# A gate left in PSUM and bf16 parts read in place, in the edge messages of a graph network

## The chip, the core and the metric

The kernel runs on one core of a Trainium2 chip. The metric is the device time of one execution in microseconds (us). The core has five engines that run side by side, each in its own order: PE (TensorE, matrix products), DVE (VectorE), ACT (ScalarE), POOL (GpSimd) and SP (SyncE, which here only issues transfers). On-chip memory is SBUF (128 partitions) and PSUM[...].

## The reference

There are 6250 nodes with 64 features and 206250 edges, sorted by their target `dst`. Four layers follow one another, each on a normalised and rectified copy of the node features `x`, each added to `x`. The first, second and fourth are convolutions over the graph. The third is the one that the change touches; cut to its core, it computes

```
Vp = leaky_relu(leaky_relu(V) @ pAw + pAb) @ pBw + pBb      # nodes
x = relu(relu(E @ mlp_w1 + mlp_b1) @ mlp_w2 + mlp_b2)       # edges
scale = sigmoid(x @ Bw + Bb)
shift = x @ Cw + Cb
msg = scale * Vp[src] + shift
M = clip(msg, EPS, None) ** 2
mean = segment_sum(M, dst) / max(count, 1)
out = sqrt(mean)
```

So each edge fetches a row of `Vp` by its source node, multiplies it by a gate (the sigmoid), adds a shift, clips, squares, and is summed into its target node.

## The kernel before

The kernel first counts the edges between all pairs of nodes into a dense matrix `A` in fp8. The convolutions are then matrix products with `A`, in which the f32 node features are split into three bf16 parts. These stages lie before and after the one of interest and are not changed.

**The stage of the messages** goes over the edges in G = 202 groups. A group is 128 x 8 edges: 128 partitions, J = 8 edges in each, D = 64 features, so that a tile of a group is 128 x 512. The function `slot(i)` writes out one step of a software pipeline, in which different groups are at different steps: group i is fetched (`fetched`, L1351) and its edge features are turned (L1358), group i - 1 goes through the first edge layer, i - 2 through the second, i - 3 through `gates_and_shifts` (L1372), i - 4 (`M_AT`) becomes messages, i - 5 is summed (`summed`, L1404), and i - 6 is added to its nodes (`added_to_nodes`, L1413). The order on PE, ACT and DVE is just the order in which the code is written (`manual_schedule`); POOL and SP are ordered by the compiler's scheduler.

The steps of a group that matter here are these:

- `fetched` has POOL issue 8 indirect transfers (L1354), each of which fetches 128 rows of `Vp` by the edges' source indices, into the tile `v`, of which there are 4.
- `gates_and_shifts` has PE write `p_bc` in PSUM, the gate's and the shift's arguments beside one another for each edge, out of biases (L1376) and products (L1380). It takes two banks and there is one such tile, so PE can't begin the next group's before this one's is read.
- `gated` has ACT write the sigmoid of the gate's half into an SBUF tile `gate` (L1385).
- `clipped` has DVE multiply `gate` by `v` (L1389), add the shift out of `p_bc` (L1390), and take the maximum with EPS (L1391). L1390 is the last reader of `p_bc`.
- `squared` has ACT square the message twice: once rounded to bf16 into the first part of `m3` (L1396), once in f32 in place (L1397).
- In `slot`, DVE then compares the targets with the lanes of a window of nodes, which gives the 0/1 matrix `to` in bf16 (L1401), and subtracts the first part from the square (L1452); ACT rounds what is left to bf16, the second part (L1453); DVE subtracts that and writes the third part (L1464).
- `summed` has PE multiply `to` by the three parts, 8 products of 128 x 192 (L1408), which sum the messages of one target node.

Beside that, DVE and PE do other work in the same slots, handed out by `some_of`: the check that `A` is symmetric (`crossed`: PE turns pieces of `A`, L1260, and DVE compares them, L1266), and the next layer's first products (`partial`: PE at L748, DVE at L1285). SP loads for it `piece` (L1246) and `there` (L1253), and for the messages the edge features `e`, four slots ahead (L1348). Where a chunk of 7 blocks of nodes is complete, `finished` (L1320) takes roots and normalises it, six times within the stage and once at its end.

Of the kernel before, what the change touches and what calls it, by code (L numbers as in the profile page):

```python
# [8 lines left out]
F32 = mybir.dt.float32  # L9
BF16 = mybir.dt.bfloat16  # L10
FP16 = mybir.dt.float16
I32 = mybir.dt.int32
AF = mybir.ActivationFunctionType
# [3 lines left out]
P = 128  # L17
N = 6250
D = 64
# [6 lines left out]
J = 8  # L26
# [590 lines left out]
def fast(ctx, tc, bad, x, src, dst, edge_attr, W3, b3, W4, b4, w1, b1, w2, b2, Bw, Bb, Cw, Cb,  # L617
         pAw, pAb, pBw, pBb, out):

    nc = tc.nc  # L620
# [135 lines left out]
    with ExitStack() as ph:  # L756
# [73 lines left out]
        with ExitStack() as ps:  # L830
            psum = ps.enter_context(tc.tile_pool(name="ps0", bufs=1, space=PSUM, reuse_waits="tile"))
            p = psum.tile([P, SG, P], F32, name="p_a", bufs=2)
            nc.tensor.transpose(p[:D, 0, :], W3_sb, ident)
            nc.vector.tensor_copy(W3T, p[:D, 0, :])
            p = psum.tile([P, SG, P], F32, name="p_a", bufs=2)
# [43 lines left out]
            for c in range(GC):  # L879
# [8 lines left out]
                p = psum.tile([P, 1024], BF16, name="p_dig")  # L888
# [6 lines left out]
                if c % 9 == 8 or c == GC - 1:  # L895
                    c0 = c // 9 * 9
                    p = psum.tile([P, 512], F32, name="p_node")
# [19 lines left out]
            p = psum.tile([P, 512], F32, name="p_node")  # L917
# [7 lines left out]
            p = psum.tile([P, 512], F32, name="p_node")  # L925
# [288 lines left out]
    with ExitStack() as ph:  # L1214
        cpool, w1_d, w2_d, b1_c, b2_c, BC, BC_b, ones, src_g, lane, own, count = made.pop()
        mpool = ph.enter_context(tc.tile_pool(name="mpool", bufs=3, reuse_waits="tile"))
# [89 lines left out]
        def read_them():  # L1306
            while read:
                read.pop(0)()

        def some_of(n):  # L1310

            for _ in range(min(n, len(todo))):
                f, *args = todo.pop(0)
                if f is not here:
                    read_them()
                then = f(*args)
                if then:
                    read.append(then)
# [23 lines left out]
        BC_AT, M_AT, SUM_AT, ADD_AT = 3, 4, 5, 6  # L1342
        of = [{} for _ in range(G)]
        ends = [e + ADD_AT for e in ends]

        def loaded(g):
            of[g]["e"] = mpool.tile([P, J * D], F32, name="e", bufs=6)
            nc.sync.dma_start(of[g]["e"], edge_attr[g * P * J:(g + 1) * P * J, :].rearrange(  # L1348
                "(p j) f -> p (j f)", j=J))

        def fetched(g):  # L1351
            v = of[g]["v"] = mpool.tile([P, J, D], F32, name="v", bufs=4)
            for j in range(J):
                nc.gpsimd.indirect_dma_start(  # L1354
                    out=v[:, j, :], out_offset=None, in_=Vp_dram[:, :],
                    in_offset=bass.IndirectOffsetOnAxis(ap=src_g[:, g, j:j + 1], axis=0))

        def turned_edges(g):  # L1358
            p = of[g]["p_e"] = ps_a.tile([P, 512], F32, name="p_e")
            e = of[g].pop("e")  # L1360
            for k in range(J // 2):
                nc.tensor.transpose(p[:, k * P:(k + 1) * P], e[:, k * P:(k + 1) * P], ident)

        def layer(g, w, x, p):
            of[g][p] = ps_a.tile([P, 512], F32, name=p)
            nc.tensor.matmul(of[g][p], w, of[g].pop(x), start=True, stop=True)  # L1366

        def evicted(g, p, t, **how):
            of[g][t] = mpool.tile([P, 512], F32, name=t)
            nc.scalar.activation(of[g][t], of[g].pop(p), **how)  # L1370

        def gates_and_shifts(g):  # L1372
            p_bc = of[g]["p_bc"] = ps_a.tile([P, J, 2, D], F32, name="p_bc")
            h2 = of[g].pop("h2")
            for b in range(2):
                nc.tensor.matmul(p_bc[:, 4 * b:4 * b + 4].rearrange("p j o f -> p (j o f)"), ones,  # L1376
                                 BC_b, start=True, stop=False)
                for k in range(2):
                    q = 2 * b + k
                    nc.tensor.matmul(p_bc[:, 2 * q:2 * q + 2].rearrange("p j o f -> p (j o f)"),  # L1380
                                     h2[:, q * P:(q + 1) * P], BC, start=False, stop=(k == 1))

        def gated(g):
            gate = of[g]["gate"] = mpool.tile([P, J, D], F32, name="gate")
            nc.scalar.activation(gate, of[g]["p_bc"][:, :, 0, :], AF.Sigmoid)  # L1385

        def clipped(g):
            m = of[g]["m"] = mpool.tile([P, J, D], F32, name="m")
            nc.vector.tensor_mul(m, of[g].pop("gate"), of[g].pop("v"))  # L1389
            nc.vector.tensor_add(m, m, of[g].pop("p_bc")[:, :, 1, :])  # L1390
            nc.vector.tensor_scalar_max(m, m, EPS)  # L1391

        def squared(g):
            m = of[g]["m"]
            m3 = of[g]["m3"] = mpool.tile([P, J, 3, D], BF16, name="m3")
            nc.scalar.activation(m3[:, :, 0, :], m, AF.Square)  # L1396
            nc.scalar.activation(m, m, AF.Square)  # L1397

        def compared_nodes(g):
            to = of[g]["to"] = mpool.tile([P, P, J], BF16, name="to")  # L1400
            nc.vector.tensor_tensor(  # L1401
                to, count, lane[:, g, :].unsqueeze(1).to_broadcast([P, P, J]), op=OP.is_equal)

        def summed(g):  # L1404
            p = of[g]["p_s"] = ps_a.tile([P, 512], F32, name="p_s")[:, :3 * D]
            m3, to = of[g].pop("m3"), of[g].pop("to")
            for j in range(J):
                nc.tensor.matmul(p, to[:, :, j], m3[:, j].rearrange("p t f -> p (t f)"),  # L1408
                                 start=(j == 0), stop=(j == J - 1))

        begun = set()
# [1 line left out]
        def added_to_nodes(g):  # L1413

            r = mpool.tile([P, D], F32, name="r_s")
            nc.vector.tensor_reduce(r, of[g].pop("p_s").rearrange("p (t f) -> p f t", f=D),
                                    axis=AX.X, op=OP.add)
            for k, (b, q0, q1) in enumerate(halves(g)):
                part = own[:, q1 if k else q0, k:k + 1]
                if b in begun:  # L1420
                    nc.vector.scalar_tensor_tensor(H[:, b, :], r, part, H[:, b, :],
                                                   op0=OP.mult, op1=OP.add)
                else:
                    nc.vector.tensor_scalar(H[:, b, :], r, part, None, op0=OP.mult)
                    begun.add(b)
            return [b // CB for b, _, _ in halves(g) if last[b] == g and b % CB == CB - 1]

        def slot(i):
            def at(later):
                return 0 <= i - later < G  # L1430

            if i + 4 < G:
                loaded(i + 4)
            if at(3):
                evicted(i - 3, "p_2", "h2", func=AF.Relu, bias=b2_c)
            if at(M_AT):
                gated(i - M_AT)
                clipped(i - M_AT)
            if at(0):
                fetched(i)  # L1440
                turned_edges(i)
            read_them()
            if at(1):
                layer(i - 1, w1_d, "eT", "p_1")
            if at(M_AT):
                squared(i - M_AT)
            n = -(-len(todo) // max(min(k for k in ends if k >= i) + 1 - i, 1))
            some_of(n - n // 2)
            if at(M_AT):
                compared_nodes(i - M_AT)  # L1450
                m, m3 = of[i - M_AT].pop("m"), of[i - M_AT]["m3"]
                nc.vector.tensor_sub(m, m, m3[:, :, 0, :])  # L1452
                nc.scalar.activation(m3[:, :, 1, :], m, AF.Copy)  # L1453
            done = added_to_nodes(i - ADD_AT) if at(ADD_AT) else []
            if at(2):
                layer(i - 2, w2_d, "h1", "p_2")
            if at(BC_AT):
                gates_and_shifts(i - BC_AT)
            if at(0):
                evicted(i, "p_e", "eT", func=AF.Copy)  # L1460
            if at(1):
                evicted(i - 1, "p_1", "h1", func=AF.Relu, bias=b1_c)
            if at(M_AT):
                nc.vector.tensor_sub(m3[:, :, 2, :], m, m3[:, :, 1, :])  # L1464
            read_them()
            some_of(n // 2)
            if at(SUM_AT):
                summed(i - SUM_AT)
            for c in done:
                finished(c)  # L1470
# [3 lines left out]
        with tc.manual_schedule(engines={ET.PE, ET.Activation, ET.DVE}):  # L1474
            for i in range(G + ADD_AT):
                slot(i)
            read_them()
# [19 lines left out]
    with ExitStack() as ph:  # L1497
# [5 lines left out]
        for layer in range(3):  # L1503
# [25 lines left out]
            else:  # L1529
                for s in range(CS):  # L1530
# [3 lines left out]
                    t = whole[:, :, s % 2 * CW:(s % 2 + 1) * CW]  # L1534
                    p = psum.tile([P, 512], F32, name="p_sum", bufs=2)
# [9 lines left out]
def gnn_kernel(tc, *args):  # L1545
    nc = tc.nc
    with tc.tile_pool(name="verdict", bufs=1) as verdict:
        bad = verdict.tile([1, 1], I32, name="bad")
        fast(tc, bad, *args)
        n = nc.values_load(bad[0:1, 0:1], min_val=0, max_val=2 ** 30)  # L1550
        with tc.If(n > 0):
            general(tc, *args)
# [31 lines left out]
```

## Time and profile before

| | us |
|---|---|
| runs of the kernel, median of 3 | 3608.37 (3608.08 to 3612.73) |
| the profiled execution | 3611.97 |
| its span, first to last instruction | 3610.2 |
| busy: PE | 3039.4 |
| busy: DVE | 1954.2 |
| busy: POOL | 1665.0 |
| busy: ACT | 1239.3 |
| first to last gather of `v` (L1354) | 1042 to 3126 |

The profile is that of one execution. "Busy" leaves out waiting and the issue of ordinary transfers, but an indirect transfer issued by POOL counts, since POOL itself works on it. [...] In a list of groups a line has: code line, engine, operation, tiles written and read, shapes, count, then busy us and mean ns, then the idle time of the engine just before and what ended it. In a timeline a line has: start, duration, engine, code line, operation, and the idle time before it. The "chain" is the work that ended last, followed back from the last instruction.

### The profile page before, as it was taken

What the parts mean: (1) busy time and instruction counts of PE and PEld (TensorE: products, weight loads), DVE (VectorE), ACT (ScalarE), POOL (GpSimd) and SP (SyncE); (2) the same over time, 40 slices, a digit from 0 to 9 for tenths busy, and PEclk for the clock granted to TensorE, in tenths of its full rate; (3) what the DMA queues carried; (4) which work ended last, traced back from release to release, by engine and by line L of the source; (5) the groups of instructions that cost most, each with busy time, mean ns of one, the idle gap of its engine ahead of it and who ended that gap; (6) DMA issues with size and microseconds to landing.
All of it is one profiled execution on the core that took longest, in us unless ns stands there. A gap on an engine that the chain in (4) does not pass through costs nothing.

```text
span 3610.2 us, 59581 instructions
## 1 busy us (share of the span) xinstructions
PE 3039.4 (84%) x24393; PEld 2141.2 (59%) x24393; DVE 1954.2 (54%) x3899; ACT 1239.3 (34%) x2024; POOL 1665.0 (46%) x1889
## 2 busy tenths in 40 slices
PE   1699999999977777878878887878887888799999
PEld 0466667999954444444444444444454444489998
DVE  6899993532235546556555655655655565531111
ACT  1577772000023434434333443434433444210000
POOL 4200001000037777777777777777777777400000
PEclk9699999999988888889889888888988888799999
DMA  3233335565532223223323232322332322256664
GB/s 107 64 91 95 95 95 189 188 205 183 178 101 80 77 53 84 71 70 97 86 68 97 70 85 79 88 68 76 91 88 70 94 70 68 81 166 194 196 206 143
DMA packets 229312, 388.76 MB, mean 108 GB/s; under 512 B 137573, under 2 KB 139743, under 8 KB 228771
## 3 DMA queue, kind: packets, MB, share of 16 engines
q1 hardware_dynamic: 170420, 321.51, 28.3%
q0 software_dynamic: 55104, 60.65, 8.3%
q8 instruction: 193, 3.16, 0.4%
q10 hardware_dynamic: 3504, 2.70, 0.3%
q14 instruction: 91, 0.75, 0.1%
HBM read 340.47 MB, written 44.24 MB: 107 GB/s over the span
## 4 chain that ended last, share of the span: by engine, by line
POOL 35%; PE 35%; issue 14%; DMA 9%; DVE 5%; ACT 1%; POOLq 0%; DVEq 0%; SPq 0%; ACTq 0%
POOL v L1354 35%; PE p_acc L1026 21%; PE p_sum L748 7%; DMA v<-Vp_dram,src_g 7%; PE p_a L861 4%; DMA near<-pairs,begin_i 1%; PE p_node L739 1%; DMA piece<-A 1%; DVE lo L852 0%; DMA run<-pairs,exact_i 0%; PE p_acc L1023 0%; PE p_node L970 0%; PE p_bc L1380 0%; DMA X<-in_x 0%; PE p_node L975 0%
## 5 line engine op out<-in xcount | busy, mean ns | idle before, releaser
L1354 POOL DMA_INDIRECT v<-Vp_dram,src_g x1616 | 1592.1, 985 | 859.9 <-issue 828.6
L1026 PE MATMUL p_acc<-U,piece 128*128 128x192 bf16 x9604 | 817.7, 246 | 5.0 <-DMA piece<-A 5.0
L1026 PEld LDWEIGHTS <-piece 128*128 128x128 fp8e4 x9604 | 798.9, 98 | 17.0 <-DMA piece<-A 5.2
L1380 PE MATMUL p_bc<-BC,h 128*128 128x256 f32 x1616 | 585.8, 496 | 0.0
L1389 DVE TENSOR_TENSOR m<-gate,v 128x512 f32<-128x512 f32 x202 | 140.3, 694 | 762.5 <-DMA v<-Vp_dram,src_g 627.7
L1380 PEld LDWEIGHTS p_bc<-BC,h 128*128 128x128 f32 x1616 | 341.2, 234 | 154.7 <-issue 116.2
L1396 ACT ACTIVATE m<-m 128x512 bf16<-128x512 f32 x202 | 127.2, 630 | 821.9 <-DVE m L1391 821.9
L748 PEld LDWEIGHTS <-U 128*64 128x64 bf16 x4116 | 231.1, 112 | 215.4 <-issue 68.3
L1036 DVE TENSOR_REDUCE zg<-p_acc 128x128 f32<-128x384 f32 x112 | 56.3, 507 | 537.4 <-PE p_acc L1026 536.9
L865 ACT ACTIVATE strip<-p_a 128x784 fp8e4<-128x784 f32 x392 | 302.3, 820 | 112.6 <-PE p_a L861 112.0
L1376 PE MATMUL p_bc<-BC_b,ones 3*128 3x512 bf16 x404 | 180.9, 448 | 167.3 <-DVE m L1390 167.2
L1260 PE MATMUL p_sum<-ident_b,piece 128*128 128x128 bf16 x1372 | 154.9, 238 | 183.7 <-DVE junk L1266 183.4
L1260 PEld LDWEIGHTS <-piece 128*128 128x128 fp8e4 x1372 | 117.7, 107 | 318.8 <-issue 301.2
L1376 PEld LDWEIGHTS <-ones 3*128 3x128 bf16 x404 | 37.5, 93 | 439.4 <-DVE m L1390 235.3
L1366 PE MATMUL p<-h,w_d 128*128 128x512 f32 x404 | 253.5, 713 | 38.6 <-ACT h L1370 38.6
L748 PE MATMUL p_sum<-piece,U 128*64 128x448 fp8e4 x2058 | 238.1, 374 | 27.0 <-DVE junk L1266 18.7
L1370 ACT ACTIVATE h<-p,b_c 128x512 f32<-128x512 f32 x404 | 255.8, 684 | 12.9 <-PE p L1366 12.6
L1266 DVE SCALAR_TENSOR_TENSOR junk<-p_sum,there 128x512 bf16<-128x512 f32 (+1 forms) x392 | 242.1, 618 | 27.3 <-PE p_sum L1260 18.7
L748 PE MATMUL p_sum<-strip,U 128*64 128x448 fp8e4 x2058 | 242.0, 359 | 2.5 <-ACT U L711 1.4
L852 DVE TENSOR_TENSOR lo<-count,key 128x2048 bf16<-128x2048 bf16 x196 | 239.6, 1222 | 0.0
L861 PEld LDWEIGHTS <-lo 128*128 128x128 bf16 x3136 | 164.7, 103 | 98.6 <-DVE lo L852 75.8
L861 PE MATMUL p_a<-hd,lo 128*128 128x98 bf16 x3136 | 195.1, 217 | 32.6 <-DVE lo L852 31.1
(198 smaller groups left out, 3308.5 us busy)
## 6 DMA issues: line engine op xcount, KB each, us to landing
piece<-A SPq DMA_DIRECT2D x249, 784.0 KB, 4.3
e<-in_edge_attr SPq DMA_DIRECT2D x202, 256.0 KB, 2.7
A<-strip SPq DMA_DIRECT2D x14, 2744.0 KB, 13.1
v<-Vp_dram,src_g POOLq DMA_INDIRECT x1616
there<-A SPq DMA_DIRECT2D x28, 784.0 KB
pairs<-pair SPq DMA_DIRECT2D x1, 1616.0 KB, 5.3
Vp_dram<-v SPq DMA_DIRECT2D x7, 224.0 KB
out<-X SPq DMA_DIRECT2D x6, 224.0 KB
```

The costliest lines, as they stand in the source:

```text
L748: nc.tensor.matmul(p[half * D:(half + 1) * D, :w], U3[:, b, k, :], at_block, start=(i < 2), stop=(i >= 3 * n - 2))
L852: nc.vector.tensor_tensor(t, of.unsqueeze(1).to_broadcast(t.shape), key[:, k, at:at + GB].rearrange("p (h j) -> p h j", j=GQ) .unsqueeze(2 ...
L861: nc.tensor.matmul(p[:, j, :2 * NB], lo[:, g // GQ, :, g % GQ], hd[:, g // GQ, :, g % GQ], start=True, stop=True)
L865: nc.scalar.activation(strips[s][:, :, col:col + 2 * SG].rearrange("p b (j l) -> p b j l", l=2), p[:, :, :2 * NB].rearrange("p j (b l) -> ...
L1026: nc.tensor.matmul(p[d // 2][:, d % 2 * 3 * D:(d % 2 + 1) * 3 * D], t[:, b, d * P:(d + 1) * P], U3[:, k * CB + b, :, :].rearrange("p t f - ...
L1260: nc.tensor.matmul(p[:, a - a0, :], held["here", i, k][:, a, b * P:(b + 1) * P], ident_b, start=True, stop=True)
L1266: nc.vector.scalar_tensor_tensor(junk[:, :(a1 - a0) * P], p[:, :a1 - a0, :].rearrange("p a q -> p (a q)"), 15.5, of_there, op0=OP.min, op1 ...
L1354: nc.gpsimd.indirect_dma_start(out=v[:, j, :], out_offset=None, in_=Vp_dram[:, :], in_offset=bass.IndirectOffsetOnAxis(ap=src_g[:, g, j:j ...
L1366: nc.tensor.matmul(of[g][p], w, of[g].pop(x), start=True, stop=True)
L1370: nc.scalar.activation(of[g][t], of[g].pop(p), **how)
L1376: nc.tensor.matmul(p_bc[:, 4 * b:4 * b + 4].rearrange("p j o f -> p (j o f)"), ones, BC_b, start=True, stop=False)
L1380: nc.tensor.matmul(p_bc[:, 2 * q:2 * q + 2].rearrange("p j o f -> p (j o f)"), h2[:, q * P:(q + 1) * P], BC, start=False, stop=(k == 1))
```

## The change

Three things are done, all in the steps of a message:

- The sigmoid is written back over its argument in `p_bc`, in PSUM, and the tile `gate` is gone. The product with `v` reads it there.
- The square is computed once, in f32, into the first of three f32 parts. Each further part is the part before it less that part's upper half. The upper 16 bits of an f32 number are a bf16 number (the f32 number cut off, not rounded); `upper` is a view that takes every second 16-bit element, and both the subtraction and the matmul read through it. The second square and the copy to bf16 on ACT are gone. The last part is also cut off by the matmul's view.
- The subtractions write f32 where the second wrote bf16, and `m3` has f32 parts, twice the size.

Where the instructions stand on each engine is otherwise kept. On SP's queue some loads of `there` come ahead of one load of `e` that they came behind.

```
         def gated(g):
-            gate = of[g]["gate"] = mpool.tile([P, J, D], F32, name="gate")
-            nc.scalar.activation(gate, of[g]["p_bc"][:, :, 0, :], AF.Sigmoid)
+            gate = of[g]["p_bc"][:, :, 0, :]
+            nc.scalar.activation(gate, gate, AF.Sigmoid)
 
         def clipped(g):
+            p_bc = of[g].pop("p_bc")
             m = of[g]["m"] = mpool.tile([P, J, D], F32, name="m")
-            nc.vector.tensor_mul(m, of[g].pop("gate"), of[g].pop("v"))
-            nc.vector.tensor_add(m, m, of[g].pop("p_bc")[:, :, 1, :])
+            nc.vector.tensor_mul(m, p_bc[:, :, 0, :], of[g].pop("v"))
+            nc.vector.tensor_add(m, m, p_bc[:, :, 1, :])
             nc.vector.tensor_scalar_max(m, m, EPS)
 
+        def upper(t):
+
+            return t.bitcast(BF16)[..., 1::2]
+
         def squared(g):
-            m = of[g]["m"]
-            m3 = of[g]["m3"] = mpool.tile([P, J, 3, D], BF16, name="m3")
-            nc.scalar.activation(m3[:, :, 0, :], m, AF.Square)
-            nc.scalar.activation(m, m, AF.Square)
+            m3 = of[g]["m3"] = mpool.tile([P, J, 3, D], F32, name="m3")
+            nc.scalar.activation(m3[:, :, 0, :], of[g].pop("m"), AF.Square)
+
+        def rest(g, k):
+            m3 = of[g]["m3"]
+            nc.vector.tensor_sub(m3[:, :, k, :], m3[:, :, k - 1, :], upper(m3[:, :, k - 1, :]))
...
-                nc.tensor.matmul(p, to[:, :, j], m3[:, j].rearrange("p t f -> p (t f)"),
+                nc.tensor.matmul(p, to[:, :, j], upper(m3[:, j].rearrange("p t f -> p (t f)")),
                                  start=(j == 0), stop=(j == J - 1))
...
                 compared_nodes(i - M_AT)
-                m, m3 = of[i - M_AT].pop("m"), of[i - M_AT]["m3"]
-                nc.vector.tensor_sub(m, m, m3[:, :, 0, :])
-                nc.scalar.activation(m3[:, :, 1, :], m, AF.Copy)
+                rest(i - M_AT, 1)
...
             if at(M_AT):
-                nc.vector.tensor_sub(m3[:, :, 2, :], m, m3[:, :, 1, :])
+                rest(i - M_AT, 2)
```

## The prediction

> **What bounds the kernel now.** First the page's slices (tenths of a slice of 90 us), its chain (shares of the span) and the costliest group:
>
> ```profile
> PE   1699999999977777878878887878887888799999
> ...
> POOL 4200001000037777777777777777777777400000
> ```
> ```profile
> POOL 35%; PE 35%; issue 14%; DMA 9%; DVE 5%; ACT 1%; POOLq 0%; DVEq 0%; SPq 0%; ACTq 0%
> ```
> ```profile
> L1354 POOL DMA_INDIRECT v<-Vp_dram,src_g x1616 | 1592.1, 985 | 859.9 <-issue 828.6
> ```
> From 1042 to 3126 us, the stage of the messages, POOL issues the 1616 gathers of `v`. By the tile's view one lasts 940 / 944 / 1476 ns (least, median, most). The 1615 gaps between them are all 303 to 315 ns, 492 us in sum: POOL never waits for a buffer. The stage is 1592 + 492 = 2084 us, and its only elastic part is 1592.1 - 1616 x 0.944 = 67 us, by which issues are longer than the median. The other engines have room (columns: PE, PEld, DVE, ACT, POOL busy us and count, PE clock, DMA share, GB/s):
>
> ```profile
> 1600.00:2000.00 400.00, 325.58 (x1679) 186.90 (x1679) 235.24 (x520) 165.64 (x281) 305.52 (x311) 0.88 0.31 83
> ```
> Of a slot of 10.3 us PE has 1.9 idle, DVE 4.2, ACT 6.0. After each of the six finished chunks L1389 starts 9 to 10.6 us after its last gather's issue, where the least is 1.8, and DVE's next slots (1389.5, 1396.8, 1404.2 in the timeline) take 7.3 us each until it has caught up: left to themselves the other engines are faster than POOL. So the question is what stretches an issue. One slot of the timeline (start, us, engine):
>
> ```profile
> 2002.28 0.69 DVE L1389 TENSOR_TENSOR m<-gate,v 128x512 f32<-128x512 f32 x1 [0.96 <-DMA v<-Vp_dram,src_g]
> ...
> 2002.47 1.32 POOL L1354 DMA_INDIRECT v<-Vp_dram,src_g  x1 [0.30 <-issue]
> ...
> 2003.07 0.69 DVE L1390 TENSOR_TENSOR m<-m,p_bc 128x512 f32<-128x512 f32 x1
> ...
> 2004.09 0.94 POOL L1354 DMA_INDIRECT v<-Vp_dram,src_g  x1 [0.30 <-issue]
> ...
> 2005.34 0.94 POOL L1354 DMA_INDIRECT v<-Vp_dram,src_g  x1 [0.30 <-issue]
> ...
> 2005.41 0.69 DVE L1401 TENSOR_TENSOR to<-count,lane 128x1024 bf16<-128x1024 bf16 x1
> 2006.02 0.68 DVE L1452 TENSOR_TENSOR m<-m,m 128x512 f32<-128x512 f32 x1
> ...
> 2006.59 0.94 POOL L1354 DMA_INDIRECT v<-Vp_dram,src_g  x1 [0.30 <-issue]
> ...
> 2007.40 0.69 DVE L1464 TENSOR_TENSOR m<-m,m 128x512 bf16<-128x512 f32 x1
> ...
> 2007.84 1.07 POOL L1354 DMA_INDIRECT v<-Vp_dram,src_g  x1 [0.30 <-issue]
> ```
> The issue at 2002.47 starts inside L1389 and ends 0.82 us after it (2002.97 + 0.82 = 2003.79); that at 2007.84 ends 0.82 after L1464. Over the stage this is a rule: an issue that starts at least 0.03 us into a DVE instruction with two SBUF inputs, with more than 0.13 of it left, ends 0.82 us after that instruction. Matched so, the 67 us belong to L1401 (23.5, 66 hits), L1389 (20.7, 81 hits), L1464 (8.8), L1452 (8.4) and short sums. L1390 and L1266, with one input in PSUM, stretch none, in either operand place.
>
> [...] these rows have 688 to 694, PSUM or SBUF:
>
> ```profile
> L1389 DVE TENSOR_TENSOR m<-gate,v 128x512 f32<-128x512 f32 x201 | 139.6, 694 | 759.6 <-DMA v<-Vp_dram,src_g 624.8 <-ACT gate L1385 134.8
> L1464 DVE TENSOR_TENSOR m<-m,m 128x512 bf16<-128x512 f32 x201 | 138.6, 690 | 6.8 <-ACT m L1453 1.4
> L1452 DVE TENSOR_TENSOR m<-m,m 128x512 f32<-128x512 f32 x201 | 138.5, 689 | 34.5 <-ACT m L1397 30.1
> L1390 DVE TENSOR_TENSOR m<-m,p_bc 128x512 f32<-128x512 f32 x201 | 138.2, 688 | 21.2 <-DVE m L1389 0.5
> ```
> [...] L861 reads its moving bf16 at step 2: 98 columns, 209 ns, against 250 for 192 (L1026) and 357 for 448 (L748) at step 1, between 200 and 700 us. The line through those two gives 211, so step 2 cost nothing.
>
> **The change, part by part.**
> *Gate in PSUM.* L1389 becomes one SBUF and one PSUM input, like L1390: 688 to 694 ns as now, and its 81 hits go: 20.7 us gross. But POOL keeps its cadence, 0.94 + 0.305 = 1.245 us, and meets the later instructions of the slot elsewhere. In the slot above, without the hit the issue ends at 2003.41 and the next start at 2003.71, 2004.96 and 2006.21. The last is now inside L1452 (to 2006.70), ends at 7.52, and the next starts at 7.82 in place of 7.84: the gain of 0.38 is given back to 0.02. I walked all 81 slots so, with DVE at its recorded times, to the next L1389: 14.1 of the 20.7 us return (L1452 7.4, L1401 5.5, L1464 0.6, the chunk's end 0.6), 6.6 stay. That is within the slot alone; what stays moves the later gathers, their landings and so the later slots. So I carried the same rule on through the 202 slots: each issue starts 305 ns after the last, each L1389 starts as long after its last issue as recorded (or, where it started on its gate, as long after the instruction before it), each later DVE instruction as long after the one before. As a check this gives 2084.6 for the stage as it was (recorded 2084.3), and 7.6 to 8.5 less without L1389's hits and L1452's waits, by how the landings are scattered. I take 8, an estimate from these recorded times.
> *ACT.* The square rounded to bf16 becomes one in f32; the second square (L1397) and the copy (L1453) go: 2 x 202 x 0.63 = 254 us of ACT. All lies under POOL's issues; with the cover gone it would be 1.26 us a slot. L1452 loses its 30.1 us of waits for L1397, L1464 1.4, again under POOL. ACT then evicts `eT` and `h1` earlier, for which PE scarcely waits. The gate's write to PSUM is shown by no row: read-PSUM-write-SBUF is 603 ns, and I keep that. 0.1 us either way moves only the 52 slots in which L1389 starts on the gate's end, not POOL.
> *Subtractions.* L1452 and L1464 keep place, size and two SBUF inputs; new are the f32 output and a bf16 input at step 2. Lower bound 688; upper unknown[...]. In the walk, 31 ns more on both costs 6 us.
> *PE.* L1408's 8 matmuls read at step 2: nothing by L861's row; at half rate, 8 x 0.08 = 0.64 us a slot, inside the 1.9 idle, and about 1 us in the tail.
> *Buffers and queues.* p_bc is still released by L1390; `m` is freed earlier. On SP's queue a few loads of `there` (L1253) move ahead of one load of `e`. SP's own waits show L1253 held by DVE's comparisons for at most 9.6 us; behind it `e` is asked for four slots, 41 us, ahead. Nothing.
> *Tail.* After the last issue (3126.3) one wait of 0.23 us of L1452 goes; the rest is PE's.
> Sum: 3611.97 (the profiled execution, span 3610.2) - 8 - 0.3 = 3603.7. The median of the runs is 3.6 below that execution; 3608.4 - 8.3 = **3600.1 us**.
>
> **Rivals.**
> *All is kept:* 3608.4 - 20.7 - 0.3 = 3587. For: in the walk 23 of the 81 slots keep over three quarters. Against: 43 keep under a quarter, as the slot shown does.
> *Nothing is left:* phases give back the rest, or L1389 is held as before: 3605 to 3612. For: 8 us is what remains of two larger sums[...]. Against the second half: L1266 (PSUM first, SBUF second, 392 instructions) never stretched an issue.
> *Slower:* the step-2 reads lengthen both subtractions, which are those that POOL meets. At 31 ns for 6 us, the gain is used up at +44 ns (733); 0.2% slower needs +80 (770), 3616 or more. [...]
>
> **How the numbers follow.** A gain of 3 to 14 us 0.60, all kept or more 0.14, nothing left 0.15, slower 0.11. A difference under 0.2% (7.2 us) is about what a measurement here can't tell from none. Faster than 3601.2: two thirds of the first and the second, with a little for gains I can't see, 0.56; slower than 3615.6: 0.08; the rest 0.36. The range 3589 to 3610 leaves out half of the second case and most of the last.
>
> **What would show it.** Right: L1389's successor has one SBUF input and no issue ends 0.82 after it; POOL's mean falls from 985 to about 980, gaps still 305; the first subtraction stretches more issues than L1452 did (8.4 to about 20 us); ACT 254 us less busy. Wrong: subtractions over 730 ns, gaps of POOL over 0.4 us (then buffers bind), or gathers still stretched by the product.

## The result: slower by 0.2%, and the profile after

The changed kernel takes 3615.55 us (median; 3608.39 to 3619.24), the kernel before 3608.61 (3603.86 to 3613.01). The ratio is 1.0018, 95% interval 1.0011 to 1.0024: slower by 6.9 us, where 8 us less was forecast. The profiled execution took 3616.26 us, 4.3 more than that of before.

The slices and the chain of the page look as they did; POOL is the bound from 1042 to 3131 us:

```profile
PE   1699999999977777878778787877888878799999
...
POOL 4200001000037777777777777777777777500000
```
```profile
POOL 36%; PE 35%; issue 14%; DMA 8%; DVE 5%; ACT 1%; POOLq 0%; DVEq 0%; SPq 0%; ACTq 0%
```

The costliest groups (busy us, mean ns of one, idle before and its releaser):

```profile
L1354 POOL DMA_INDIRECT v<-Vp_dram,src_g x1616 | 1596.7, 988 | 860.0 <-issue 828.0
...
L1390 DVE TENSOR_TENSOR m<-p_bc,v 128x512 f32<-128x512 f32 x202 | 139.7, 692 | 830.1 <-DMA v<-Vp_dram,src_g 728.7
...
L1404 DVE TENSOR_TENSOR m<-m 128x512 f32<-128x512 f32 x404 | 277.3, 686 | 4.0 <-ACT m L1400 3.8
...
L1385 ACT ACTIVATE p_bc<-p_bc 128x512 f32<-128x512 f32 x202 | 117.7, 583 | 394.8 <-PE p_bc L1380 393.5
```

A gather's issue lasts 988 ns in the mean, 3 more than before, which makes 4.6 us over the 1616. Both subtractions (now one line, L1404) last about what they did, 686, and wait for ScalarE 3.8 us in all, where L1452 alone waited 30.1. The longest issue is still 1.47 us, the gaps are still at most 0.315, and what follows the stage is unchanged (483.9 us before, 483.2 after). So the stage, 2084.3 us before and 2088.8 after, answers for all that sets the two profiled executions apart. (The medians differ by more, since the execution profiled before was 3.4 us above its median, the one after 0.7.)

Line numbers after: sigmoid L1385, product L1390, addition L1391, maximum L1392, square L1400, both subtractions L1404, comparison L1408, the sum's matmuls L1415.

Here is the loss in the slot of one group of edges (start, us, engine), first in the kernel before:

```profile
1987.66 0.69 DVE L1389 TENSOR_TENSOR m<-gate,v 128x512 f32<-128x512 f32 x1 [1.86 <-ACT gate L1385]
...
1990.05 0.69 DVE L1401 TENSOR_TENSOR to<-count,lane 128x1024 bf16<-128x1024 bf16 x1
1990.30 0.63 ACT L1397 ACTIVATE m<-m 128x512 f32<-128x512 f32 x1
1990.72 0.94 POOL L1354 DMA_INDIRECT v<-Vp_dram,src_g  x1 [0.30 <-issue]
1990.96 0.69 DVE L1452 TENSOR_TENSOR m<-m,m 128x512 f32<-128x512 f32 x1 [0.22 <-ACT m L1397]
```

The same slot in the changed kernel:

```profile
1991.78 0.69 DVE L1390 TENSOR_TENSOR m<-p_bc,v 128x512 f32<-128x512 f32 x1 [1.84 <-ACT p_bc L1385]
...
1993.75 0.63 ACT L1400 ACTIVATE m<-m 128x512 f32<-128x512 f32 x1 [2.00 <-DVE m L1392]
...
1994.11 0.68 DVE L1408 TENSOR_TENSOR to<-count,lane 128x1024 bf16<-128x1024 bf16 x1
...
1994.71 0.68 DVE L1404 TENSOR_TENSOR m<-m 128x512 f32<-128x512 f32 x1
...
1994.80 1.41 POOL L1354 DMA_INDIRECT v<-Vp_dram,src_g  x1 [0.30 <-issue]
```

In both an issue starts about 3.0 us after the product. Before, the first subtraction waits for the second square and starts 3.30 us after the product, 0.24 us behind that issue, which takes its usual 0.94. After, there is no second square to wait for; the subtraction starts right behind the comparison, 2.93 us after the product and 0.09 us ahead of the issue, and holds it to 1.41: the issue ends 0.82 us after it (1995.39 + 0.82 = 1996.21).

The same matching as in the prediction (an issue belongs to the DVE instruction that ends 0.82 us before it) gives for the whole stage, in us by which issues are longer than 0.943:

| kernel | stage | product | 1st subtraction | 2nd | comparison | maximum | all |
|---|---|---|---|---|---|---|---|
| before | 2084.3 | 20.7 | 8.4 | 8.8 | 23.5 | 0.1 | 68.2 |
| after | 2088.8 | 0 | 30.7 | 9.3 | 24.7 | 2.8 | 72.8 |

The product's 20.7 us are gone, as the change's first part should have it. 22.3 came in at the first subtraction. In the kernel before it never started sooner than 3.30 us after the product, since it waited for the second square (L1397). In the changed kernel it starts less than 3.2 us after the product in 101 of the 202 slots (10% of all start at 2.83 or sooner). All 101 are slots in which it waited before, and what it stretches in them went from 5.0 to 17.6 us. In the other slots it went from 3.5 to 13.1 us; that part is not the lost wait's alone, since the kernel e5 below, which keeps the wait, has 11.5 us in them. Issues whose start falls in the subtraction's first 0.3 us: 7 before, 74 after.

### The profile page after: what moved, and what is told of

Its sections match the earlier page's. It is cut to its first block, busy times and chain, and to the rows that moved or that the text cites. A ratio compares the mean times of both kernels' runs of the same rounds, so it can differ in the third digit from the quotient of the medians.

```text
span 3614.4 us, 59375 instructions
## 1 busy us (share of the span) xinstructions
PE 3037.1 (84%) x24393; PEld 2140.6 (59%) x24393; DVE 1944.6 (54%) x3899; ACT 1005.2 (28%) x1620; POOL 1670.5 (46%) x1889
## 4 chain that ended last, share of the span: by engine, by line
POOL 36%; PE 35%; issue 14%; DMA 8%; DVE 5%; ACT 1%; POOLq 0%; DVEq 0%; SPq 0%; ACTq 0%
POOL v L1354 35%; PE p_acc L1026 21%; PE p_sum L748 7%; DMA v<-Vp_dram,src_g 6%; PE p_a L861 4%; PE p_node L739 1%; DMA near<-pairs,begin_i 1%; DMA piece<-A 1%; DVE lo L852 0%; DMA run<-pairs,exact_i 0%; PE p_acc L1023 0%; PE p_node L970 0%; PE p_bc L1380 0%; DMA X<-in_x 0%; PE p_node L975 0%
## 5 line engine op out<-in xcount | busy, mean ns | idle before, releaser
L1390 DVE TENSOR_TENSOR m<-p_bc,v 128x512 f32<-128x512 f32 x202 | 139.7, 692 | 830.1 <-DMA v<-Vp_dram,src_g 728.7
L1400 ACT ACTIVATE m<-m 128x512 f32<-128x512 f32 x202 | 127.2, 630 | 922.9 <-DVE m L1392 922.9
L1370 ACT ACTIVATE h<-p,b_c 128x512 f32<-128x512 f32 x404 | 266.8, 684 | 100.3 <-PE p L1366 99.7
L1404 DVE TENSOR_TENSOR m<-m 128x512 f32<-128x512 f32 x404 | 277.3, 686 | 4.0 <-ACT m L1400 3.8
L1266 DVE SCALAR_TENSOR_TENSOR junk<-p_sum,there 128x512 bf16<-128x512 f32 (+1 forms) x392 | 241.7, 617 | 26.1 <-DMA e<-in_edge_attr 10.5
L1385 ACT ACTIVATE p_bc<-p_bc 128x512 f32<-128x512 f32 x202 | 117.7, 583 | 394.8 <-PE p_bc L1380 393.5
```

The source lines that it names most:

```text
L1266: nc.vector.scalar_tensor_tensor(junk[:, :(a1 - a0) * P], p[:, :a1 - a0, :].rearrange("p a q -> p (a q)"), 15.5, of_there, op0=OP.min, op1 ...
L1404: nc.vector.tensor_sub(m3[:, :, k, :], m3[:, :, k - 1, :], upper(m3[:, :, k - 1, :]))
```

## Experiments

Four accounts had to be told apart: the lost wait of the first subtraction for the second square; the gate's gain given back in full; SyncE's changed order of loads; ScalarE's work itself. The edits are against the kernel named. The quantities in the expectations are those of the table above.

### The two parts alone: e1, e2, and again e5, e6

e1 and e5 are the kernel before with the gate in PSUM:

```
-            gate = of[g]["gate"] = mpool.tile([P, J, D], F32, name="gate")
-            nc.scalar.activation(gate, of[g]["p_bc"][:, :, 0, :], AF.Sigmoid)
+            gate = of[g]["p_bc"][:, :, 0, :]
+            nc.scalar.activation(gate, gate, AF.Sigmoid)
...
-            nc.vector.tensor_mul(m, of[g].pop("gate"), of[g].pop("v"))
+            nc.vector.tensor_mul(m, p_bc[:, :, 0, :], of[g].pop("v"))
...
```

e2 and e6 are the changed kernel with these lines put back.

> The kernel before with only the gate in PSUM; squares, copy and subtractions as before. Theory A (two edits of opposite sign: the gate gains, the parts lose because the first subtraction no longer waits for the second square and slides onto POOL's issues): no issue stretched by the product (20.7 us before), the first subtraction stretches more (8.4 to about 20 us), the stage some 4 to 8 us shorter, 3601 to 3605 us. Theory B (taking the product's hits away is itself what loses, since they reset POOL's cadence): 3612 to 3618, first subtraction about 30 us. Theory C (the changed order of loads on SP's queue delays landings): this kernel keeps that order, so it equals the kernel before less the gain, 3595 to 3601.

> The changed kernel with the gate back in SBUF: only the parts are new. Theory A: the product still stretches about 20 us of issues, the first subtraction rises from 8.4 to 20 to 30 us, total 3615 to 3622. Theory B: 3606 to 3611, as before. Theory C: about 3615, with landings later than before and the product's hits as before.

Chips differ. e1 and e2 ran on one on which the kernel before takes 4157.95 us. There the gate alone gave 1.0043 (1.0019 to 1.0068) and the parts alone 1.0078 (1.0048 to 1.0109), but the bound is another. POOL's waits in e1 (us in total, times, longest):

```profile
POOL v L1354 <- issue: 805.3, 1416, 367.8
POOL v L1354 <- DVE m L1390: 563.1, 92, 17.5
```

At 92 of the 202 groups POOL waits for the product to free a buffer of `v`, 563 us in all; in the profiles of about 3600 us it never does. TensorE's granted clock from 1042 to 3000 us is 0.77, against 0.86 in the profile before. These runs tell nothing of the 6.9 us. The same two kernels on a chip where the kernel before takes 3610.89:

> The gate-only kernel once more, in the hope of a chip on which the kernel before takes about 3608 us and POOL never waits for a buffer (the first chip of the experiments took 4158 us, and POOL waited at 105 of the 202 groups). There, theory A: 3601 to 3605, product stretches no issue, first subtraction about 20 us. Theory B: 3612 to 3618, first subtraction about 30 us. Theory C: 3595 to 3601.

> The parts-only kernel once more, for the same reason. Theory A: product about 20 us as before, first subtraction 20 to 30 us, 3615 to 3622. Theory B: 3606 to 3611. Theory C: about 3615 with later landings.

The gate alone: 3607.28 us, 0.9990 (0.9984 to 0.9997). The parts alone: 3623.45 us, 1.0036 (1.0022 to 1.0050). The sum of the two, +9.0 us, is near what the change cost. The gathers' group in e5, then in e6:

```profile
L1354 POOL DMA_INDIRECT v<-Vp_dram,src_g x1616 | 1587.7, 983 | 859.9 <-issue 820.6
```
```profile
L1354 POOL DMA_INDIRECT v<-Vp_dram,src_g x1616 | 1604.0, 993 | 860.0 <-issue 822.8
```

So here the loss is in the parts, not in the gate. In e6 the first subtraction again starts early (10% at 2.72 us or sooner) and stretches 28.3 us of issues; in e5, where it still waits, it never starts before 3.23 and stretches 18.8. The product isn't later behind its gathers in e6, which has the changed order of loads, than in e5, which has the old one: 5% of the slots start within 1800 and 1802 ns of their last issue's end. So SyncE's order of loads shows no delay of the landings.

### The second square put back: e7

Against the changed kernel; the parts are still read in place and the gate is in PSUM:

```
-            nc.scalar.activation(m3[:, :, 0, :], of[g].pop("m"), AF.Square)
+            nc.scalar.activation(m3[:, :, 0, :], of[g]["m"], AF.Square)
+            nc.scalar.activation(of[g]["m"], of[g]["m"], AF.Square)
...
-            nc.vector.tensor_sub(m3[:, :, k, :], m3[:, :, k - 1, :], upper(m3[:, :, k - 1, :]))
+            whole = of[g].pop("m") if k == 1 else m3[:, :, 1, :]
+            nc.vector.tensor_sub(m3[:, :, k, :], whole, upper(m3[:, :, k - 1, :]))
```

> The changed kernel with the second square on ACT put back (the first subtraction takes it as its whole, so that it waits for ACT as before the change; the copy to bf16 stays gone). If the parts lose because the first subtraction slid forward: it starts 3.23 us or later after the product again, its hits fall from 30.7 to about 19 us, and the time is that of the gate alone, 3603 to 3610. If the loss lies in the step-2 reads, the f32 parts or the missing copy: 3613 to 3620.

3602.60 us, 0.9979 (0.9972 to 0.9987) of before: an instruction more on ScalarE in each slot, and quicker than both kernels. One line of DVE's waits (us, times, longest), and the gathers' group:

```profile
DVE m L1406 <- ACT m L1401: 30.0, 75, 0.8
```
```profile
L1354 POOL DMA_INDIRECT v<-Vp_dram,src_g x1616 | 1583.4, 980 | 860.0 <-issue 834.0
```

The 30 us of waits are back, no first subtraction starts before 3.2 us, and it stretches 14.6 us of issues in place of 30.7. The changed kernel wasn't run beside it, so each is read against the kernel before of its own measurement: 6.9 us slower and 8.8 quicker.

### The first subtraction later: e10

The changed kernel with the first subtraction moved behind the addition to the nodes, with no wait and no work added:

```
             if at(M_AT):
                 compared_nodes(i - M_AT)
-                rest(i - M_AT, 1)
             done = added_to_nodes(i - ADD_AT) if at(ADD_AT) else []
+            if at(M_AT):
+                rest(i - M_AT, 1)
```

> The changed kernel with the first subtraction moved behind the addition to the nodes on DVE (0.6 to 0.9 us later, same instructions, same durations). If only the place against POOL's cadence matters: the time moves by 3 to 15 us, either way, and by as much as the sum of the stretched issues moves (72.8 us in the changed kernel), with the rest of the stage unchanged at 2016 us. If the time comes from the work itself: within 2 us of the changed kernel's 3615.6.

3610.82 us, 0.9997 (0.9989 to 1.0005): most of the loss gone, against the kernel before on e7's chip. The first subtraction stretches 8.5 us, but the second, now right behind it, 18.0. SyncE's order of loads is that of the changed kernel.

### Parts with the square, gate in SBUF (e12), and the square unread (e13, e18 beside e17)

e12 is e6 with e7's edit.

> The parts read in place, the gate in SBUF as before, and the second f32 square put back, so that the first subtraction waits for ScalarE again. If the whole loss of the parts alone (12.6 us) is the lost wait: no difference from the kernel before within 3 us, ratio 0.999 to 1.001, the first subtraction never sooner than 3.2 us after the product's start and stretching 6 to 12 us of issues, the product still 18 to 22 us. If the f32 parts themselves, or the matmuls' step of 2, cost something as well: 1.002 to 1.003.

3603.89 us, 0.9988 (0.9980 to 0.9997), a little better than expected: the first subtraction stretches 7.1 us, as expected, and the product only 14.5, which was not. So reading the parts in place shows no cost once the subtraction waits. But e7 and e12 bring back three things at once: the wait, ScalarE's work and (in e7 wholly) the order of loads. e13 brings back the work alone. Against e7:

```
-            whole = of[g].pop("m") if k == 1 else m3[:, :, 1, :]
-            nc.vector.tensor_sub(m3[:, :, k, :], whole, upper(m3[:, :, k - 1, :]))
+            nc.vector.tensor_sub(m3[:, :, k, :], m3[:, :, k - 1, :], upper(m3[:, :, k - 1, :]))
```

> The changed kernel with the second square put back on ScalarE, as in e7, but read by nobody: the first subtraction takes the first square twice, as in the changed kernel, and doesn't wait for the second. ScalarE has e7's work, SyncE's order of loads is that of the changed kernel. If it was the lost wait: the first subtraction is as early as in the changed kernel (from 2.8 us after the product's start), stretches 26 to 32 us of issues, and the time is 3612 to 3618 us, ratio 1.001 to 1.0025. If ScalarE's own work or its later evictions made e7 quicker: 3600 to 3606, ratio 0.9975 to 0.999.

3607.62 us, 0.9993 (0.9985 to 1.0002): neither answer. The first subtraction is as early as in the changed kernel, yet stretches only 23.3 us. Its chip differed: 5% of the products start within 1784 ns of the last issue's end, against 1843 in the profile after. The changed kernel, e13's and e7's on one chip:

> The changed kernel itself, beside the next two on one chip, because the product starts 1784 to 1877 ns (5% of the slots) after its last gather's issue by the chip on which a run landed, and e13 had the least. If the loss belongs to the kernel: 1.001 to 1.0025, first subtraction about 30 us. If it hangs on where a chip's landings put the product within an issue (e13's chip had the most products 200 to 300 ns into an issue, with 168 ns of stretch a slot, the changed kernel's 300 to 400 ns in, with 425): by the chip, 0.9985 to 1.0025.

> e13 again, beside the changed kernel on one chip. If the lost wait alone makes the loss: as e14 within 0.05%. If ScalarE's own work matters too: below e14 by 0.1 to 0.25%.

> e7 again, beside the changed kernel on one chip. If the lost wait makes the loss: 0.2 to 0.4% below e14, as before (3602.6 against 3615.6), first subtraction about 15 us, and below e15 by as much.

That chip was like e1's, the kernel before takes 4152.24 us there: 1.0003 (0.9984 to 1.0021), 1.0014 (0.9988 to 1.0039) and 1.0042 (1.0019 to 1.0066), POOL again waiting for the product, 555 and 577 us in e14 and e15. No answer, except that where POOL is not the bound e7's gain isn't there. Two of them on another chip:

> The changed kernel, to be set beside the next on one chip; e14 and e15 fell on a chip where the kernel before takes 4152 us and another bound holds, and told nothing of this. If the loss belongs to the kernel: 1.001 to 1.0025 and about 30 us at the first subtraction. If it hangs on where a chip's landings put the product: anything from 0.9985 to 1.0025.

> The second square put back and read by nobody. If the lost wait alone makes the loss: as e17 within 0.05%, with the first subtraction within 3 us of e17's. If ScalarE's own work matters too: below e17 by 0.1 to 0.25%, with the first subtraction 5 to 10 us less.

The changed kernel takes 3617.06 us, 1.0020 (1.0010 to 1.0029), the one with the unread square 3616.92, 1.0021 (1.0014 to 1.0028). The gathers in e17, then in e18:

```profile
L1354 POOL DMA_INDIRECT v<-Vp_dram,src_g x1616 | 1598.1, 989 | 860.0 <-issue 829.2
```
```profile
L1354 POOL DMA_INDIRECT v<-Vp_dram,src_g x1616 | 1599.1, 990 | 860.0 <-issue 833.2
```

With all of ScalarE's work back and no wait, nothing is won (first subtraction 30.6 and 28.1 us). On the same chip e12, with the work and the wait, had 3603.89, 13 us less, although its gate is in SBUF, which by e5 is the slower place. So ScalarE's work is not what counts; the lost wait is.

e13 is the exception. It is the same kernel as e18, and has 0.9993 on its chip and 1.0021 on this one: a chip can move a kernel by as much as the whole loss, and no two runs on different chips settle anything here. What carries the conclusion is that it comes out alike on three other chips, each time against the kernel before beside it: with the wait 0.9990, 0.9979 and 0.9988 (e5, e7, e12), without it, and the subtraction early, 1.0036, 1.0020 and 1.0021 (e6, e17, e18).

What differs between e13 and e18 can be seen in where the product starts within an issue of POOL. In e18, 54 slots have it 0.3 to 0.4 us into one, and their issues are stretched by about 450 ns a slot; in e13, 57 slots have it 0.2 to 0.3 us in, with 168 ns. The two stages differ by 12 us, with products 0.08 us apart by the 5% figure (1784 and 1866 ns). That the changed kernel itself would have lost nothing on e13's chip is an inference; it wasn't run there.

### Stretching taken away: e3 and e9, e4 and e8, e11

e3 and e9 leave both subtractions out: the second and third part are mere copies of the first, by ScalarE.

```
-            nc.vector.tensor_sub(m3[:, :, k, :], m3[:, :, k - 1, :], upper(m3[:, :, k - 1, :]))
+            nc.scalar.activation(m3[:, :, k, :], m3[:, :, k - 1, :], AF.Copy)
```

> The changed kernel with both subtractions left out: ACT copies the part instead (parts 2 and 3 are then copies of part 1). If the loss lies in POOL's issues held by the two subtractions (30.7 + 9.3 us in the changed kernel): no hits from them, the comparison of nodes keeps 24.7 to 35, stage 30 to 40 us shorter, 3575 to 3587. If POOL's stretch only moves to whatever DVE instruction is there: 3605 to 3615. If ACT's load matters, later than 3615.

> The changed kernel with both subtractions left out and copies on ACT in their place, on such a chip: their 40 us of hits go, the comparison keeps 24.7 to 35: 3575 to 3587. If the holds only move to other DVE instructions: 3605 to 3615.

e3, on the first chip: 4164.97 us, 1.0015 (0.9995 to 1.0035). e9: 3583.66 us, 0.9924 (0.9909 to 0.9939). Of the 40.0 us that both subtractions stretch in the changed kernel, 29.4 stay won in the stage (2088.8 to 2059.4, on two chips); the comparison stretches 31.6 in place of 24.7.

e4 and e8 cut the subtractions and the comparison into four pieces each, the changed kernel else:

```
-            nc.vector.tensor_sub(m3[:, :, k, :], m3[:, :, k - 1, :], upper(m3[:, :, k - 1, :]))
+            for j in range(0, J, J // 4):
+                s = slice(j, j + J // 4)
+                nc.vector.tensor_sub(m3[:, s, k, :], m3[:, s, k - 1, :], upper(m3[:, s, k - 1, :]))
...
```

> The changed kernel with each of the three DVE instructions with two SBUF inputs (comparison of nodes and both subtractions) cut into four: same work, each piece about 0.29 in place of 0.69 us. By the rule a hit needs more than 0.16 us, and its wait is at most the piece's end: hits fall from 65 to some 18 us over the stage, POOL's mean from 988 to about 958 ns, 3560 to 3575, while DVE is busy 280 us more. If DVE's fixed time per instruction or its place behind PE counts, gaps of POOL above 0.4 us appear and the time is 3615 or more.

> The changed kernel with the comparison of nodes and both subtractions cut into four each, on a chip where POOL never waits for a buffer: hits of the three fall from 65 to about 18 us, stage 2030 to 2045 us, 3560 to 3575. If a hit costs the same whatever the length of the instruction: 3612 or more. If DVE becomes the bound: POOL gaps over 0.4 us.

e4, on the first chip: 4174.37 us, 1.0044 (1.0023 to 1.0064). e8: 3597.57 us, 0.9966 (0.9954 to 0.9978), a third of the gain that was expected. A piece of a subtraction takes 0.28 us alone, four in a row 0.89. A slot of e8's timeline shows why:

```profile
2009.51 0.89 DVE L1406 TENSOR_TENSOR m<-m 128x128 f32<-128x128 f32 x4
2009.93 1.29 POOL L1354 DMA_INDIRECT v<-Vp_dram,src_g  x1 [0.30 <-issue]
```

The issue starts as the third of four pieces begins and ends 0.82 us after the fourth (2010.40): here it did not get in between pieces that follow one another without a gap.

e11 is e7 with the row of node numbers that the comparison reads put into PSUM, so that it has one input in SBUF:

```
+        p_s_all = ps_a.tile([P, 512], F32, name="p_s")
+        count_p = p_s_all[:, 3 * D:3 * D + P]
+        nc.vector.tensor_copy(count_p, count[:, :, 0])
...
-                to, count, lane[:, g, :].unsqueeze(1).to_broadcast([P, P, J]), op=OP.is_equal)
+                to, count_p.unsqueeze(2).to_broadcast([P, P, J]),
+                lane[:, g, :].unsqueeze(1).to_broadcast([P, P, J]), op=OP.is_equal)
...
-            p = of[g]["p_s"] = ps_a.tile([P, 512], F32, name="p_s")[:, :3 * D]
+            p = of[g]["p_s"] = p_s_all[:, :3 * D]
```

> The kernel with the second square and the gate in PSUM (3602.6 us), and the row of node numbers that the comparison reads is f32 in PSUM, so that the comparison has one input in SBUF. If an instruction with one input in PSUM never holds POOL's issues: the comparison stretches none (27.5 us there), something under half of it comes back at the two subtractions, so 3575 to 3592 us, although the comparison itself may take 1.0 to 1.2 us in place of 0.69. If the longer comparison makes the slot longer than POOL's (gaps of POOL over 0.4 us)[...]: 3603 or more.

3596.01 us, 0.9966 (0.9952 to 0.9979), 4 us over the expected range. The comparison and the gathers:

```profile
L1413 DVE TENSOR_TENSOR to<-p_s,lane 128x1024 bf16<-128x1024 f32 x202 | 246.0, 1218 | 0.5 <-PE p_s L1421 0.2
```
```profile
L1357 POOL DMA_INDIRECT v<-Vp_dram,src_g x1616 | 1573.7, 974 | 859.8 <-issue 829.1
```

It lasts 1218 ns in place of 0.69 us and stretches no issue: 27.5 us less than in e7. But 15.3 of them turn up at the subtractions (21.9 to 37.2) and 2.6 at the maximum: two thirds come back at the other instructions that POOL meets (e7's profile is of another chip).

All of it in one table, in us (e13 to e18 as above; stage = 2016 us + all):

| kernel | stage | product | 1st sub. | 2nd sub. | comparison | maximum |
|---|---|---|---|---|---|---|
| e5 gate alone | 2079.9 | 0 | 18.8 | 11.4 | 21.8 | 3.4 |
| e6 parts alone | 2096.2 | 13.5 | 28.3 | 11.6 | 21.5 | 0.1 |
| e12 parts, second square | 2076.6 | 14.5 | 7.1 | 6.4 | 26.9 | 0 |
| e7 both, second square | 2075.6 | 0 | 14.6 | 7.3 | 27.5 | 3.5 |
| e10 first subtraction later | 2083.0 | 0 | 8.5 | 18.0 | 26.1 | 4.2 |
| e17 changed kernel | 2090.3 | 0 | 30.6 | 9.6 | 25.2 | 3.6 |
| e18 square unread | 2091.3 | 0 | 28.1 | 9.5 | 29.1 | 3.3 |
| e13 the same, other chip | 2078.9 | 0 | 23.3 | 9.8 | 19.2 | 3.8 |
| e9 no subtractions | 2059.4 | 0 | | | 31.6 | 4.3 |
| e11 comparison from PSUM | 2065.8 | 0 | 26.9 | 10.3 | 0 | 6.1 |

## Why the prediction was wrong, step by step

**The bound: right.** The stage is still 1616 issues with gaps of 0.303 to 0.317 us, and in every run at about 3600 us the stage is 2016 us plus what the issues are stretched.

**The rule of 0.82 us: right, but not complete.** It left the maximum out: one SBUF input, 427 ns (median) for 512 f32 elements where an instruction with two inputs takes 687, no hits to speak of before (0.1 us). After, 2.8 us: 29 issues that start 0.05 to 0.28 us into it end 0.81 to 0.82 us after it. What in the maximum makes the hits isn't shown. Why they came only now can be read from the starts. Before, an issue that the product held ended 0.82 us after the product, and the next one began 0.3 us later, which is 0.3 us into the maximum: 80 issues began there, and none in the maximum's first 0.28 us. Without the product's hold 32 begin in that first stretch, and the maximum stretches 29. It is also held itself, before as after: 58 and 68 of the 202 last over 0.45 us, up to 0.68, all 58 and 64 of the 68 where an issue had started 0.45 to 0.76 us before.

**Gate in PSUM: right in sign, half in size.** The product's hits went from 20.7 us to none. The walk kept 8; the gate alone kept 3.6 (0.9990, which is 1.1 to 5.8), and e7 is 4.0 us further below the kernel before than e12, which differs from it in the gate. What came back came mainly at the first subtraction: 10.4 us, where the walk of the slots had put 7.4, 2.6 at the second (walk 0.6) and 3.3 at the maximum, where it had none; at the comparison, where the walk had 5.5, the issues' stretch went down by 1.7.

**"L1452 loses its 30.1 us of waits ... again under POOL": this is the step that failed.** DVE's time was indeed under POOL; but that wait was what held the first subtraction behind the issue that starts about 3 us after the product. Costed at nothing, its loss cost 12.6 us by the parts alone (1.0036, 7.9 to 18 us). e6 shows the loss, e7 and e12 that it goes with the wait back, e18 that the work without the wait doesn't remove it, e10 that moving the subtraction without a wait removes most of it. The prediction did name the first subtraction as the one that would stretch more, 8.4 to about 20 us; it was 30.7.

**The walk carried through the 202 slots: its 8 us are those of the product's hits alone.** The prediction says "without L1389's hits and L1452's waits". The rule carried out again on the profile before gives 2084.5 us for the stage as it was (recorded 2084.3), and 7.5 to 8.6 less without the product's hits, which is the forecast's 7.6 to 8.5. Without the waits alone it gives 12 to 13 us more, about what e6 lost; without both, 1 to 5.5 more. All of these are estimates from the recorded times of the profile before. So the walk as described would have warned of the loss; as far as can be told, the waits had stayed in it. The agreement of 2084.6 with 2084.3 couldn't show that, since it tested the kernel before alone. Nor is the walk exact: on the changed kernel's own profile it gives 2087 us for a recorded 2088.8 (2089 to 2090 with the maximum counted in), but in that last form 2079 to 2086 with the product starts of other profiles put in.

**Subtractions: right.** 685 and 687 ns, f32 output and step 2 included, against 690, the forecast's estimate (its four rows have 688 to 694). So the rival "slower" had the sign but not the cause.

**ACT, PE, tail: right.** ScalarE's busy time fell from 1239.3 to 1005.2 us, 234 (forecast 254); its write of the gate to PSUM takes 583 ns, not 603. The matmuls that read at step 2 take 273 ns in the mean, 275 before (median 252 and 246; they overlap: after, the eight at 2005.51 take 0.89 us together), inside PE's idle time. The forecast's half rate, 0.08 us more for each, was an estimate; between its two rows at step 1, 256 columns make 107 ns, so 192 make 80. What follows the stage moved by 0.7 us.

**SyncE's order of loads: no sign of a cost.** e5 has the old order and e6 the new one on one chip, and the product starts no later in e6; e9, the quickest of all, has the new order. It wasn't tried alone.

**The rivals.** "Nothing is left" (3605 to 3612) stopped short, and the case that happened, a lost wait that moves an instruction into the bound engine's way, was in none of them: it had been put into the sum as a nothing.

## What to carry to other kernels

Where one engine sets the pace with a fixed cadence (here a gather every 1.245 us, 0.94 + 0.305, where nothing stretches it), and others hold it only when they meet it, a wait on an engine with room is not free to remove: it also fixes where the next instructions fall. Here that was worth more than the gain that was sought: 13 us between e12 and e17, against about 4 for the gate in PSUM. Before costing such a wait at nothing, list where each instruction that can hold the bound engine starts within its cadence, with and without the wait. When a hold is taken away at one of several such instructions, expect part of it back at the others: of 20.7, 27.5 and 40.0 us taken away in e5, e11 and e9 the stage kept 4.4, 9.8 and 29.4 (by profiles of different chips). And run a walk that is to price a change once for each term that it is said to hold: a sum that doesn't move when a term is taken out doesn't hold it.

## What the runs showed that was not expected

- The maximum, an f32 tensor_scalar from SBUF to SBUF, and an issue of a gather lengthen one another: after, 29 issues that start in its first 0.28 us, 2.8 us in all, and 64 maxima that start 0.45 to 0.76 us into an issue, which last over 0.45 us, up to 0.68, against a median of 0.43. A hold can also hide another: while the product held issues, none met the maximum's first 0.28 us.
- An issue that meets instructions with two SBUF inputs back to back can wait for all of them (1.29 us in e8, four pieces of 0.89 us together).
- Behind the product with one input in PSUM the addition starts 726 ns after the product's start (median, after), behind the one with both in SBUF 797 (before).
- On two chips the same kernel before takes 4152 and 4158 us, 15% more. It wasn't profiled there; its variants were, with TensorE's clock at 0.76 to 0.77 from 1042 to 3000 us and POOL waiting 555 to 589 us for buffers. On the first of them the change measured 1.0003 (0.9984 to 1.0021). What sets these chips apart stays open.
